# Layer 0 of a four-layer pre-activation network: where signed results, streamed statistics and weight preparation live and when they run

## The chip, the core and the metric

The kernel runs on one core of a Trainium2 chip. A core has five engines with an instruction stream of their own each: TensorE (PE, matmuls), VectorE (DVE), ScalarE (ACT), GpSimd (POOL) and SyncE (SP). SP and POOL also issue DMA transfers here, each in the order of its own stream. The metric is the device time of one execution in microseconds (us); the kernel before takes 2870.44 us, the median of three runs (2867.19 to 2876.09).

## The reference

The input `x` has shape (1024, 16, 16, 16), float32: batch, height, width, channel. Four layers follow, each `x = x + f(gn(x))`, where `gn` normalises over height, width and the two channels of each of eight groups:

- layer 0: `f` is a tensor-train product with three cores, a linear map from the 4096 values of one sample to 4096 values;
- layers 1 and 3: `f` is a cellular-automaton update: two fixed 3 x 3 depthwise filters, a dense layer from 48 to 128 with relu, a dense layer back to 16, and a mask from a 3 x 3 maximum;
- layer 2: `f` is a 3 x 3 convolution with 16 channels in and out, plus a bias.

All of the change lies in the code of layer 0 and in the preparation of later layers' weights, which runs beside layer 0.

## The kernel before

**Data.** The batch is worked on in two chunks of 512. Two big tiles in the on-chip memory, `XN[0]` and `XN[1]` (128 partitions x 32 lines x 512 values), take turns; `flats` are the same tiles as flat rows of 16384 values. The running sum of the network lies in DRAM as `xf[0]` and `xf[1]`, one for each chunk.

**Layer 0 as 13 pairs.** The tensor-train product is written as 13 pairs of smaller products (`OUTER`, a fast block-matrix scheme), numbered 0 to 12. Pair j has four units, q = 0 to 3, and each unit seven inner products (`INNER`) in two halves: 14 steps in a unit, 56 in a pair. One step is four float32 matmuls 128 x 128 x 256 at L1538, which the profile shows as two records each, so a pair has 448 such records. The order of work inside a unit is written out by hand in `pieces` (L1517): after given steps the code emits `store(u - 1)`, the VectorE operations that mix weight blocks (`mix`, L1454), `build(u + 1, h)` (L1427: PE matmuls at L1439 that make the next unit's weights, copied out by ACT at L1444) and `gload(u + 2, h)` (L1400: the DMA loads for the build after that, on SP). `gather` (L1568) adds the results of an inner product into the unit's tile `r`, on ACT (L1580, L1582) and VectorE (L1574, L1584). There are two places for `r`, so one unit's results are stored while the next unit's are gathered.

**Store.** `store(u)` (L1481) sends a unit's results to the places of `xf` where the scheme needs them, with signs: some as they are, some negated or as a sum of both results with signs. The latter are first made into a tile of the pool `t4`, by ACT (L1498) or VectorE (L1505, L1507). From the second time that a place of `xf` is written, the DMA accumulates and is issued by POOL (L1512); the first goes through SP (L1514).

**The part.** The input of pair p, its part, lies in tile `XN[p % 2]`: values 0 to 8191 hold lines that `part_steps` (L1192) builds during pair p - 1 from blocks in DRAM, fetched in pieces of two lines into `t4` (L1255), two pieces ahead, but one ahead for part 11 and none for part 12 (`deep`, L1219). Values 8192 to 14335, three eighths of the tile and here called its third, hold three sums of those lines. `combined` (L1162) makes them: five sums in two halves, ten VectorE operations (L1178). For the pairs in `late` (L2064: 1, 2, 4, 6, 8, 10, 12) they are woven into the first ten steps of the pair itself; for the others they run at the end of the pair before.

So when the next pair is in `late`, the third of the other tile stays unused for the whole of a pair. The weight preparation (`nca_weights`, L228) works in such a third: `rooms` (L2007) is the third of `XN[0]` for both sets.

**The pool `t4`.** Four tiles of 128 x 1024 float32, given out in turn. In layer 0 it serves the fetched pieces, the signed results, the pieces of the statistics, and the room of the filter weights. A tile that is asked for is written only when the users of its last content are done, a DMA out of it included.

**Beside a pair.** `run` (L1958) emits the 56 steps of a pair, and between them the callables of several lists ("spans"). Each span has a start and an end as a fraction of the pair; a bare number in the list is idle time in us of an assumed pair of 107 us, held to at most 0.7 of the span, and the rest is shared out to the callables by their costs. This fixes the place of every instruction in each engine's stream; on the chip each engine runs its stream in order and waits where data are missing. The lists beside pair j are:

- `part_steps(j + 1)`, from 0.04 to 0.78;
- `aside[j]`: weight set 1 in pair 3, its folding in pair 5, set 3 in pair 7, its folding in pair 9, the convolution's filter weights in pair 8, statistics in pairs 10 and 11;
- `share[j]` of the 32 residual steps (L1316): POOL accumulates 512 KB of the input from `xr` into `xf` (L1319).

**Statistics.** `ahead(kind, q, root)` (L883) reads a quarter of `xf[0]` back in four pieces (L890): kind 0 sums the pieces on VectorE (L906, L909), lets PE average (`pmean`, L806), ACT copy (L917) and SP store the mean to DRAM (`means`, L918); kind 1 fetches the mean (L894), subtracts it (L897), squares on ACT (L900), sums, and lets PE make the variance (`pvar`, L922). The loads are two pieces ahead. `roots_ahead` (L945) makes the reciprocal roots and spreads them (`pr`, L950). Pair 12 then loads `xf[0]` as the next layer's input and applies both.

**Weights.** A set (`inputs` to `store`, L254 to L331) is a chain of small DMAs on POOL, a few matmuls and POOL copies, ending in the stores of `L_conv_pk` and `L_conv_kp`. Folding (`fold`, L380) has 22 steps: matmuls (L403), ACT copies into one of three tiles (L409), and sends to DRAM, half of them on POOL and half on SP (L415). `conv_weights` (L440) issues 42 small DMAs on POOL in one block (L457, L465, L468) and spreads the result 60 us later.

Of the kernel before, what the change touches and what calls it, by code (L numbers as in the profile page):

```python
# [13 lines left out]
AF = mybir.ActivationFunctionType  # L14
# [7 lines left out]
P = 128  # L22
# [83 lines left out]
def conv_preact_kernel(ctx: ExitStack, tc: tile.TileContext, a: dict, out: bass.AP):  # L106
# [333 lines left out]
    def conv_weights():  # L440
# [3 lines left out]
        room = work([P, 2, NB], "t4", "convn").rearrange("p a b -> p (a b)")  # L444
# [4 lines left out]
        V.memset(room[:, 0:448], 0.0)  # L449
        V.memset(hw, 0.0)  # L450
        f = a["L2_conv_filters"]
        with nc.allow_non_contiguous_dma(reason="weights"):
            for w in range(8):
# [7 lines left out]
            for wh in range(2):  # L461
                for y in range(3):
                    for e in range(2):
                        r0 = 32 * (y + e)
                        G.dma_start(hn[r0 + wh : r0 + 32 : 2, wh, e], f[y, 2 - 2 * wh])  # L465
            for m in range(4):
                for v in range(2):
                    G.dma_start(  # L468
                        b2[32 * m + v : 32 * m + 32 : 2], a["L2_conv_bias"].unsqueeze(1)
                    )  # L470
# [7 lines left out]
        return spread  # L478
# [404 lines left out]
    def ahead(kind, q, root):  # L883

        st = {}
        rows = slice(32 * q, 32 * q + 32)

        def load(w):
            st[w] = work([P, 2, NB], "t4", "piece")
            nc.sync.dma_start(st[w], xf[0][w : w + 2, q].rearrange("w p b -> p w b"))  # L890

        def fetch():
            st["m"] = work([P, NB], "s", "m")
            nc.sync.dma_start(st["m"], means[q])  # L894

        def centre(w):
            V.tensor_tensor(  # L897
                st[w], st[w], st["m"].unsqueeze(1).broadcast_to([P, 2, NB]), ALU.subtract
            )
            A.activation(st[w], st[w], AF.Square)  # L900

        def add(w):
            x = st.pop(w)
            if w == 0:
                st["s"] = work([P, NB], "s", "s1s")
                V.tensor_tensor(st["s"], x[:, 0], x[:, 1], ALU.add)  # L906
                return
            for i in range(2):
                V.tensor_tensor(st["s"], st["s"], x[:, i], ALU.add)  # L909

        def mean():
            st["p"] = psum([P, NB], "pmean")
            average(st["p"], gm_cw, st["s"])

        def keep_mean():
            m = work([P, NB], "s", "m")
            A.copy(m, st["p"])  # L917
            nc.sync.dma_start(means[q], m)  # L918

        def var():  # L920
            st["v"] = psum([P, NB], "pvar")
            T.matmul(  # L922
                st["v"][rows], gv_cw.rearrange("p f j -> p (f j)"), st["s"], start=True, stop=True
            )

        def keep_var():
            if "ve" not in root:
                root["ve"] = work([P, NB], "n", "ve")
            V.tensor_scalar(root["ve"][rows], st["v"][rows], GN_EPS, None, ALU.add)

        def centred_too(w):
            return [(1.2, lambda: centre(w)), 1.5] if kind else []

        steps = [(0, fetch)] if kind else []
        steps += [(0, lambda: load(0)), (0, lambda: load(2)), 4]
        for w in (0, 2, 4, 6):
            steps += centred_too(w) + [(1.3 if w else 0.7, lambda w=w: add(w))]
            if w < 4:
                steps.append((0, lambda w=w: load(w + 4)))
            steps.append(1)  # L940
        if kind:
            return steps + [1, (0.6, var), 1, (0.4, keep_var)]
# [1224 lines left out]
```

## Time and profile before

| | |
|---|---|
| median of three runs | 2870.44 us (2867.19 to 2876.09) |
| the profiled execution, its own time | 2871.32 us |
| its span, first to last instruction | 2869.6 us |
| granted TensorE clock, mean | 0.978 |
| busy share of the span: PE, VectorE, ACT, POOL | 95%, 70%, 44%, 18% |
| layer 0's thirteen pairs | 47.1 to 1686.8 us |
| pairs 2 to 12, us each | 114.9, 124.9, 132.3, 130.2, 108.1, 110.6, 118.8, 132.1, 158.2, 125.5, 105.7 |

A line of a stretch gives its bounds and length, then for each engine the busy time and, in brackets, the number of instructions, then the granted clock (1.00 is full), the mean busy share of the 16 DMA engines and GB/s. A line of waits reads: engine, tile and line that waited; what it waited for; us in total, number of waits, longest. "SPq" is SyncE's DMA queue. A busy PE is a modelled figure, so a stretch is best judged by its length.

### The profile page before, as it was taken

The numbers are of one execution on the slowest core, as the hardware profiler recorded it, in microseconds if no ns is written. First come the engines' busy times: TensorE is split into PE (matmuls) and PEld (weight loads), VectorE is DVE, ScalarE is ACT, GpSimd is POOL, SyncE is SP. The second block draws the span as 40 slices with busy tenths as digits, with TensorE's granted clock in tenths as the row PEclk, the third lists the DMA queues.
The fourth block names the chain that finished last, engine by engine and source line by source line (L and its number), as shares of the span: only waits on it lengthen the run. The fifth ranks groups of instructions, "written<-read, shape, count | busy, mean of one in ns | idle before, by whom it ended". The sixth has DMA issues, their size and how long they took to land.

```text
span 2869.6 us, 48201 instructions
## 1 busy us (share of the span) xinstructions
PE 2722.4 (95%) x19342; PEld 1771.9 (62%) x19342; DVE 1999.9 (70%) x2440; ACT 1268.9 (44%) x2139; POOL 525.8 (18%) x666
## 2 busy tenths in 40 slices
PE   6998999879999999998898999999999999999997
PEld 5877888768788878876777863343333333333444
DVE  8595667656778767555676868757877777766654
ACT  3323222122432222341232236666768657676664
POOL 2000014622421454221011101111112221110000
PEclk8999999989999999999999999999999999999998
DMA  6685678898975687978576855456566867454665
GB/s 247 218 321 192 227 162 201 169 238 188 240 172 147 172 187 163 223 169 240 159 198 144 238 145 128 100 124 156 109 148 133 196 99 193 101 99 105 171 177 202
DMA packets 261536, 502.21 MB, mean 175 GB/s; under 512 B 29285, under 2 KB 96921, under 8 KB 252097
## 3 DMA queue, kind: packets, MB, share of 16 engines
q1 hardware_dynamic: 178896, 340.88, 35.7%
q0 software_dynamic: 82224, 158.12, 32.7%
q8 instruction: 153, 2.51, 0.4%
q14 instruction: 71, 0.57, 0.1%
q10 hardware_dynamic: 192, 0.13, 0.0%
HBM read 280.66 MB, written 223.35 MB: 176 GB/s over the span
## 4 chain that ended last, share of the span: by engine, by line
PE 72%; DMA 10%; DVE 9%; issue 5%; POOL 2%; ACT 1%; SPq 1%; DVEq 0%; POOLq 0%; ACTq 0%
PE po L1538 30%; PE ph L1945 20%; PE po L1774 8%; PE po L1629 5%; PE pw L1439 4%; DMA xf<-r 1%; DMA piece<-xf 1%; DMA xn<-xn 1%; DVE xn L1178 1%; DMA xf<-neg 1%; DVE xn L1149 1%; DMA xn<-in_x_dram 1%; DMA xf<-xr 1%; PE po L1638 1%; PE L_conv_pe L403 1%
## 5 line engine op out<-in xcount | busy, mean ns | idle before, releaser
L1538 PE MATMUL po<-xn,s 128*128 128x256 f32 x3328 | 774.7, 390 | 48.9 <-DVE s L1469 17.8
L1948 ACT ACTIVATE hid<-ph,pack 128x512 f32<-128x512 f32 (+1 forms) x1040 | 641.7, 684 | 312.9 <-PE ph L1945 253.6
L1538 PEld LDWEIGHTS po<-xn,s 128*128 128x128 f32 x3328 | 639.7, 195 | 165.7 <-issue 24.7
L1538 PE MATMUL po<-xn,w 128*128 128x256 f32 x2496 | 574.3, 385 | 4.5 <-DVE xn L1178 4.5
L1538 PEld LDWEIGHTS po<-xn,w 128*128 128x128 f32 x2496 | 471.9, 192 | 86.4 <-issue 10.3
L1945 PE MATMUL ph<-xn,wq 32*128 32x512 f32 (+1 forms) x3752 | 518.1, 590 | 1.9 <-DVE u L1786 1.5
L1444 ACT COPY w<-pw 128x512 f32<-128x512 f32 x416 | 213.6, 600 | 475.4 <-PE pw L1439 379.3
L1945 PEld LDWEIGHTS ph<-xn,wq 32*128 32x128 f32 x3752 | 233.8, 184 | 228.7 <-issue 209.8
L1469 DVE TENSOR_TENSOR s<-w 128x1024 f32<-128x1024 f32 x208 | 252.5, 1222 | 50.1 <-PE po L1538 46.8
L1945 PE MATMUL ph<-xn,pack 32*128 32x512 f32 x1288 | 273.7, 607 | 5.8 <-DVE u L1786 1.6
L1774 PE MATMUL po<-hid,pack 128*32 128x512 f32 (+1 forms) x2080 | 256.0, 592 | 0.8 <-ACT hid L1948 0.5
L1786 DVE SCALAR_TENSOR_TENSOR u<-po,pack,xn 128x512 f32<-128x512 f32 (+1 forms) x130 | 96.4, 741 | 168.1 <-PE po L1774 167.0
L1828 POOL DMA_DIRECT2D xf<-u x96 | 81.9, 853 | 619.4 <-DVE u L1826 587.0
L1178 DVE TENSOR_TENSOR xn<-xn 128x1024 f32<-128x1024 f32 x130 | 154.2, 1219 | 35.1 <-DMA L_conv_kp<-xn 35.1
L744 DVE TENSOR_TENSOR xn<-xn,m 128x1024 f32<-128x1024 f32 x128 | 150.3, 1219 | 34.7 <-ACT m L767 34.6
L1945 PEld LDWEIGHTS ph<-xn,pack 32*128 32x128 f32 x1288 | 115.0, 184 | 91.3 <-issue 63.4
L1629 PE MATMUL po<-xn,convw 128*128 128x512 f32 x368 | 163.6, 598 | 0.0
L1774 PEld LDWEIGHTS po<-hid,pack 128*32 128x32 f32 x2080 | 53.9, 109 | 174.9 <-ACT hid L1948 87.1
L1439 PE MATMUL pw<-R,gq 32*128 32x128 f32 x3328 | 144.5, 286 | 8.5 <-DVE small L1091 7.9
L1439 PEld LDWEIGHTS pw<-R,gq 32*128 32x128 f32 x3328 | 116.7, 188 | 43.4 <-issue 39.6
L1574 DVE TENSOR_TENSOR r<-r,po 128x1024 f32<-128x1024 f32 x78 | 95.0, 1218 | 69.5 <-PE po L1538 60.4
L1217 DVE TENSOR_TENSOR xn<-xn,piece 128x1024 f32<-128x1024 f32 x96 | 116.2, 1220 | 34.8 <-DMA piece<-xb 34.8
(222 smaller groups left out, 2814.6 us busy)
## 6 DMA issues: line engine op xcount, KB each, us to landing
xn<-xf SPq DMA_DIRECT2D x96, 512.0 KB
xn<-xb SPq DMA_DIRECT2D x36, 1024.0 KB
wq<-L_conv_wy SPq DMA_DIRECT2D x192, 192.0 KB
piece<-xb SPq DMA_DIRECT2D x64, 512.0 KB
xf<-xn POOLq DMA_DIRECT2D x48, 512.0 KB, 9.8
xf<-neg POOLq DMA_DIRECT2D x48, 512.0 KB, 9.7
xf<-r POOLq DMA_DIRECT2D x48, 512.0 KB, 11.4
xf<-u POOLq DMA_DIRECT2D x96, 256.0 KB, 4.2
```

The source lines that it names most:

```text
L744: V.tensor_tensor(part, part, m().unsqueeze(1).broadcast_to([P, 2, NB]), op)
L1178: V.tensor_tensor(out, y, z, f)
L1217: V.tensor_tensor(y, y, x(), ALU.add if sign > 0 else ALU.subtract)
L1439: T.matmul(pw[r][:, v, i], g[rows, P * (2 * v + i) : P * (2 * v + i) + P], R[rows, k], start=k == 0, stop=k == len(gs) - 1,)
L1444: A.copy(w.rearrange("p b s t m -> p (b s t) m")[:, :, 32 * r : 32 * r + 32].rearrange("p k (v o) -> p v k o", v=2), pw[r].rearrange("p v ...
L1469: V.tensor_tensor(t.rearrange("p s t m -> p (s t m)"), x, y, f)
L1538: T.matmul(po[:, i], matrix(u, what)[:, i, t], x, start=t == 0, stop=t == 3)
L1629: T.matmul(st["po", h][wh], conv["fw"][:, y], X[:, 16 * wh + h + y - 1], start=y == max(0, 1 - h), stop=y == min(2, S - h),)
L1774: T.matmul(po[32 * j : 32 * j + 32], nca["w1"][:, v], hid[j], start=v == 0, stop=v == 1)
L1786: V.scalar_tensor_tensor(u, po, nca["b1"], X[:, 8 * q + w2, cols(hf)], ALU.add, ALU.add)
L1945: T.matmul(ph, w, x, start=k == 0, stop=k == len(tiles) - 1)
L1948: A.activation(h, ph, AF.Relu, bias=nca["bt"][:, r : r + 1])
```

## The change

- `sent(u)` is new. In pairs 3, 4 and 5, for q = 0 to 2, a signed result is made in one of six slots of 1024 values in the third of the other tile instead of a `t4` tile. In other pairs, and for q = 3 (whose store falls into the next pair), it stays in `t4`.
- `late` holds all pairs from 1 to 12; nothing is combined at the end of a pair any more, and `part_steps` ends at 0.80.
- `rooms` are now both thirds; weight set 1 is prepared in pair 2 in the third of `XN[1]`, until 0.85, and folded in pair 6, until 0.92; set 3 stays in pair 7, in `XN[0]`, until 0.85, and is folded in pair 9, until 0.92.
- `conv_weights` works in the third of `XN[1]` in pair 8 and issues its DMAs in 19 steps with 2 us of idling after each.
- `ahead` takes all jobs of a pair at once. Pieces go through six slots in the third of the other tile, loaded three ahead across the jobs; each job adds its pieces into its first one and halves that at the end; the mean or variance of a job is taken after six entries of the next job's list.
- `gload` issues its narrow loads, eight for each half of a unit's weights and needed for pair 11 alone, on POOL instead of SP.
- `deep` is gone: pieces of every part are fetched two ahead.
- The residual steps are shared out anew: 3, 0, 3, 1, 4, 3, 1, 1, 2, 4 in pairs 2 to 11 and the last ten in pair 12 (before: 3, 3, 3, 2, 2, 2, 2, 3, 4, 4 and four).

```diff
-        room = work([P, 2, NB], "t4", "convn").rearrange("p a b -> p (a b)")
...
+        steps = [clear] + [lambda w=w: main(w) for w in range(8)]
+        steps += [lambda wh=wh, y=y: edge(wh, y) for wh in range(2) for y in range(3)]
+        steps += [lambda m=m: bias(m) for m in range(4)]
+        return [x for step in steps for x in (step, 2)] + [8, spread]
...
-    def ahead(kind, q, root):
...
-        def load(w):
-            st[w] = work([P, 2, NB], "t4", "piece")
-            nc.sync.dma_start(st[w], xf[0][w : w + 2, q].rearrange("w p b -> p w b"))
...
+    def ahead(jobs, root, room):
+        slots = [
+            room[:, 2 * NB * i : 2 * NB * i + 2 * NB].rearrange("p (w b) -> p w b", w=2) for i in range(6)
+        ]
+        todo = [(kind, q, w) for kind, q in jobs for w in (0, 2, 4, 6)]
+        def load(i):
+            if i < len(todo):
+                _, q, w = todo[i]
+                nc.sync.dma_start(slots[i % 6], xf[0][w : w + 2, q].rearrange("w p b -> p w b"))
...
+            def add(x):
+                V.tensor_tensor(first, first, x, ALU.add)
+            def last():
+                st["s"] = work([P, NB], "s", "s1s")
+                V.tensor_tensor(st["s"], first[:, 0], first[:, 1], ALU.add)
...
+            for i in range(i0, i0 + 4):
+                x = slots[i % 6]
+                if kind:
+                    steps += [(1.2, lambda x=x: centre(x)), 1.5]
+                if i > i0:
+                    steps.append((1.2, lambda x=x: add(x)))
+                if i == i0 + 3:
+                    steps.append((0.8, last))
+                steps += [(0, lambda i=i: load(i + 3)), 0.7]
...
+        steps = [(0, lambda i=i: load(i)) for i in range(3)] + [6]
+        end = []
+        for n, (kind, q) in enumerate(jobs):
+            body, more = job(kind, q, 4 * n)
+            steps += body[:6] + end + body[6:]
+            end = more
+        return steps + [5] + end
...
-        deep = {NP - 2: 1, NP - 1: 0}.get(j, 2)
...
-                            queue.dma_start(
-                                g[row : row + 16], g_dram[0][l % 2, q, h, o, l // 2]
-                            )
+                            G.dma_start(g[row : row + 16], g_dram[0][l % 2, q, h, o, l // 2])
...
+        def sent(u):
+            j, q = units[u]
+            if j not in (3, 4, 5) or q == 3:
+                return work([P, 2, NB], "t4", "neg")
+            st["sent"] = at = (st.get("sent", 0) + 1) % 6
+            lo = 8192 + 2 * NB * at
+            return flats[1 - j % 2][:, lo : lo + 2 * NB].rearrange("p (s n) -> p s n", s=2)
...
-                    have[c] = t = work([P, 2, NB], "t4", "neg")
+                    have[c] = t = sent(u)
...
-    rooms = [flats[0][:, 8192:14336]] * 2
+    rooms = [x[:, 8192:14336] for x in flats]
...
-        nca_weights(name, room) for name, room in zip(("L1_conv_", "L3_conv_"), rooms)
+        nca_weights(name, room) for name, room in zip(("L1_conv_", "L3_conv_"), rooms[::-1])
...
-        late = (1, 2, 4, 6, 8, 10, 12)
+        late = range(1, NP)
...
-        share = {2: 3, 3: 3, 4: 3, 5: 2, 6: 2, 7: 2, 8: 2, 9: 3, 10: 4, 11: 4, 12: 4}
+        aside = {
+            2: (set1, 0.85),
+            6: (fold1, 0.92),
+            7: (set3, 0.85),
+            8: (conv_weights(rooms[1]), 0.9),
+            9: (fold3, 0.92),
+            10: (ahead([(0, 0), (0, 1), (0, 2), (0, 3), (1, 0), (1, 1)], root, rooms[1]), 0.96),
+            11: (ahead([(1, 2), (1, 3)], root, rooms[0]) + roots_ahead(root), 0.96),
+        }
+        share = {2: 3, 4: 3, 5: 1, 6: 4, 7: 3, 8: 1, 9: 1, 10: 2, 11: 4}
```

## The prediction

> **What bounds the kernel now.** The page first: TensorE carries the chain that ended last, and the idle time in front of layer 0's main matmul is small.
>
> ```profile
> PE 72%; DMA 10%; DVE 9%; issue 5%; POOL 2%; ACT 1%; SPq 1%; DVEq 0%; POOLq 0%; ACTq 0%
> L1538 PE MATMUL po<-xn,s 128*128 128x256 f32 x3328 | 774.7, 390 | 48.9 <-DVE s L1469 17.8
> ```
>
> Then the stretches, one per pair (here pairs 3, 4, 6, 7, 8, 10, 11, 12), cut where a pair's first L1538 starts.
>
> ```profile
> core 0: us, PE busy (x) PEld busy (x) DVE busy (x) ACT busy (x) POOL busy (x), PEclk, DMA share, GB/s
> 440.40:565.30 124.90, 115.84 (x718) 96.70 (x717) 89.55 (x105) 29.33 (x54) 71.56 (x101) 0.96 0.88 196
> 565.30:697.60 132.30, 113.60 (x769) 96.77 (x768) 81.07 (x81) 29.02 (x52) 29.64 (x29) 0.91 0.86 199
> ...
> 827.80:935.90 108.10, 107.30 (x705) 92.21 (x704) 100.40 (x95) 26.17 (x49) 14.17 (x12) 1.00 0.68 176
> 935.90:1046.50 110.60, 110.60 (x717) 93.50 (x716) 74.71 (x93) 25.29 (x49) 58.74 (x93) 1.00 0.76 161
> 1046.50:1165.30 118.80, 112.37 (x769) 96.01 (x768) 89.57 (x94) 27.73 (x51) 42.77 (x62) 0.97 0.80 194
> ...
> 1297.40:1455.60 158.20, 129.44 (x909) 104.27 (x908) 104.40 (x117) 36.22 (x61) 14.84 (x13) 0.91 0.66 182
> 1455.60:1581.10 125.50, 118.18 (x718) 95.56 (x718) 87.98 (x103) 36.05 (x61) 17.07 (x15) 0.97 0.73 184
> 1581.10:1686.80 105.70, 104.88 (x641) 90.20 (x639) 91.93 (x84) 21.00 (x40) 14.62 (x13) 1.00 0.71 180
> ```
>
> Pairs 6 and 7 show the floor: 108.1 us for 705 matmuls without a gap. Another small weight-build matmul costs 0.035 us (pair 2: 898 in 114.9 us; (114.9 - 108.1)/193). Floors then: pair 3 110.6 (as pair 7, which also prepares a weight set), pairs 4 and 8 110.3, pair 10 118.5 and pair 11 112.1 (statistics matmuls at about 0.3 us), pair 12 105.9. Excess over floor: **14.3, 22.0, 8.5, 39.7, 13.4 us** in pairs 3, 4, 8, 10, 11, together 97.9 us. That is all this change can give back; PE idle time and its half-clock tails are both in it.
>
> What ends the waits in pairs 3 and early 4:
>
> ```profile
> DVE xn L1178 <- DMA L_conv_kp<-xn: 24.6, 1, 24.6
> ...
> ACT neg L1498 <- DVE xn L1217: 19.5, 1, 19.5
> ACT neg L1498 <- DMA xf<-neg: 17.3, 1, 17.3
> ...
> PE po L1538 <- ACT xn L1582: 15.1, 2, 11.2
> ...
> PE po L1538 <- DMA xf<-neg: 7.5, 1, 7.5
> ```
>
> ACT stands in front of a negated result because its t4 tile is still a piece not yet added (19.5), or a store not yet landed (17.3); the gathers behind it in ACT's order release PE late (15.1). VectorE waits 24.6 us to overwrite the third of the tile in which weight set 1 still has stores. In pair 10, the waits of the DMA queue SP and then of the engines:
>
> ```profile
> SPq L918 <- ACT m L917: 56.4, 4, 16.6
> ```
>
> ```profile
> PE pmean L806 <- DVE s1s L909: 19.0, 3, 9.3
> ...
> DVE piece L897 <- DMA piece<-xf: 12.6, 1, 12.6
> ...
> DVE s1s L906 <- DMA piece<-xf: 10.2, 1, 10.2
> ```
>
> SP stands 56.4 us in front of storing a mean; the next job's pieces are behind it, so VectorE sums late and PE waits for the sum.
>
> **The Trainium skill.** "Perfetto Trace Analysis", Optimization Strategy: the same gap repeating can mean that there isn't enough SBUF for the next tile; three pmean waits, up to 9.3 us, fit. "DMA: Bandwidth & Descriptors", Anatomy of one DMA: a semaphore wait is spent on the issuing sequencer before dispatch; SPq L918 shows it. Same page, Issuing engines are not separate DMA queues: moving issues frees sequencer time, not engines; no run here isolates it. "TensorE: Matmul & The Clock Gate", Part 1: an idle window of about 3.4 us halves the clock; pairs 4 and 10 at 0.91 agree, about 0.09 x 132.3 = 12 us of clock in pair 4 besides the gap.
>
> **The change, part by part.**
> Signed results in the idle third, pairs 3 to 5, q 0 to 2. Pair 3 makes three per unit, pair 4 one, pair 5 two; without q 3, which stays in t4, that is 9 + 3 + 6 = 18 moved. No instruction is added. Both ACT waits above (19.5 and 17.3) lose their t4 cause, and pair 4's pieces have t4 to themselves. Next in line is the second buffer of a unit's results: ACT waited 8.2 us (one L1580 wait on DMA xf<-xn) because POOL's stores were late; they are late because of set 1, which also leaves. The last slots must have landed before the next pair's sums write there: issued near step 44 of 56, six stores took 22 us from issue to the last landing in pair 3 (484 to 506), so about step 55; the write is at step 3 of the next pair, some 8 us later.
> Weight set 1 from pair 3 to 2, ending at 0.85 instead of 0.97 (set 3 too). Pair 2 takes set 1's 2.5 us of PE from pair 3: zero sum. POOL loses 57 DMAs of set 1 (51 in pair 3, six early in pair 4) and three accumulations there. The planner gives each of the set's ten callables an equal share of what idling leaves, 0.83 x 0.30 / 10 = 0.025 of the pair, so the storing step comes at 0.825, step 47 of 56, instead of 0.97 - 0.031, step 53: 12 us earlier, with less ahead of it; the 24.6 us wait and the 10.5 us one in pair 8 should vanish. POOL in pair 2 has 12 stores, set 1, three accumulations: much as pair 7, which shows no gap. I take 2 us of new waits, between 0 and 10.
> Fold 1 from pair 5 to 6, with 4 accumulations. 88 matmuls move, zero sum. Behind an accumulation waiting for a landing on POOL stand fold sends, and ACT's copies wait for their three tiles: 2 us, between 0 and 8.
> Combined lines always in the pair's own start (new in 3, 5, 7, 9, 11). Ten VectorE sums, 12.2 us (1.22 each), move to the first ten steps (about 20 us), which also hold three mixes and the gathers. Pairs 6 and 12 start so already and PE waits 0.8 us: 1.2 us each, at most 5. VectorE afterwards: pair 3 has 89.6 + 12.2 less set 1's 6, about 96 of 110, and pair 11 88.0 + 12.2 - 0.9, about 99 of 112; pair 6 ran 100.4 of 108.1 with 0.8 us of gap.
> Statistics streamed through six slots. Per job VectorE adds 3 x 1.22 + 0.69 = 4.35 instead of 7 x 0.69 = 4.8. Five pieces are on the way when SP stops at a mean, against none; the mean stands two sums later. 24 pieces of 512 KB remain. DMA was busy 0.66 x 158.2 = 104 us; two accumulations fewer (3.1 us each: POOL's queue in pair 12 took 40 us for 13) leave 98 of 121, share 0.81, as in pair 8. SP still stops at each mean until ACT has copied it, but what is next late is then the mean's place on PE, not the data. Excess left: 6 us in pair 10, between 2 (as pair 2) and 25 (pieces land 9 us after issue, as from 1306 to 1315, and every job waits for one: 6 x 4).
> Pair 11. Loads for its builds (64 small DMAs) go from SP to POOL: 64 x 0.5 = 32 us of POOL's issue (the filter loads take 0.49 to 0.84 each), hidden in POOL's idle 250 us of two pairs. With them goes SP's wait for the matmuls that free the weight buffer (L1423, 23.4 us in four waits, longest 12.6), now POOL's: behind it stand accumulations and the next unit's stores, and for those the second result buffer gives a unit, 27 us. Cost taken as nothing; bounds: a gain of 3 us where SP's pieces come sooner, a loss of 5; without the cover see the third rival. Pair 12's pieces are fetched two ahead. But its first 20 us now hold the sums (12.2), centring and adding (4 x 1.22) and three quarters of a unit's mixes and gathers (of 5 x 1.22 + 3 x 1.22 + 2 x 0.69 = 11), 25 us of VectorE: excess 8 instead of 13.4, between 3 and 16.
> Filter weights in pair 8, in steps, out of t4: the 42 DMAs stood in one block on POOL and PE never waited for them; nothing, 1 us either way. Six more accumulations in pair 12: 6 x 3.1 = 19 us raise DMA from 75 to 94 of 105.7; X0's 16 loads are needed one per 5.5 us and come at 2.7: nothing, up to 5.
>
> Sum: excess after 2 (pair 3), 2 (4), 1.5 (8), 6 (10), 8 (11) = 19.5, so 78.4 gained; costs 3 x 1.2 (pairs 5, 7, 9) + 2 + 2 = 7.6. Net 70.8. The profiled execution took 2871.3 us (span 2869.6), 0.9 above the median of 2870.44: 2871.3 - 70.8 = 2800.5, **2799.6 against the median**.
>
> **Rivals.** Streams starve (0.12): 24 pieces in 120 us come too late; pair 10 and 11 keep 40 of their 53 us: gain 78.4 - 26 - 7.6 = 45, 2826 us. For it: pieces took 9 us to land (1306 to 1315); against: SP runs ahead into six slots. POOL congestion moves (0.09): pairs 2 and 6 get pair 3's waits (14 and 22 us): 2799.6 + 32 = 2832. For it: in the trace POOL waits, in order, for the eighth DMA before, so eight are in flight at most; against: pair 7. Slower (0.05): build loads on POOL. They are issued about 12 steps, 23 us, before their build; POOL landings took up to 21 us in pair 3, 6 to 19 in pairs 10 and 11. Eight builds late by x us each cancel 71 us at x = 9, that is at landings above 32 us; at x = 11, 2887 us. It does nothing (0.03): if the ACT and SP waits only uncover equal DMA waits: 2870.
>
> **How the numbers follow.** Likeliest case 0.71: gain 45 to 98, own range 2773 to 2826, value 2799.6. Reaching to most of the two weaker gains gives 2770 to 2838. 0.3% (8.6 us) is about what a measurement can tell from no change. Faster 0.71 + 0.12 + 0.09 = 0.92, same 0.03, slower 0.05.
>
> **What would show it.** Right: pairs 3, 4, 8 within 3 us of floor, no L1178 wait on L_conv_kp, no ACT neg wait over 5 us; pair 10 at 121 to 128 with PEclk near 1.00. Wrong: pmean or pvar waits of over 3 us remain; PE waits on ACT in pairs 2 or 6; weight builds (L1439) in pair 11 waiting for gq; pair 12 above 110.

## The result, and the profile after

The changed kernel takes **2829.64 us** (median of four runs, 2823.28 to 2831.96) against 2871.5 us before: ratio 0.985, 95% interval 0.9828 to 0.9873, a gain of 42 us. The forecast gain was 71 us. The profiled execution took 2831.96 us, its span is 2830.1 us.

The page of the changed kernel, chain shares by engine and the main matmul's group (L1538 of before is L1563 here):

```profile
PE 77%; DVE 10%; DMA 6%; issue 4%; ACT 1%; SPq 1%; DVEq 0%; ACTq 0%; POOLq 0%
L1563 PE MATMUL po<-xn,s 128*128 128x256 f32 x3328 | 768.0, 388 | 36.2 <-DVE s L1485 31.4
```

POOL is gone from the chain (2% before) and the idle time ahead of the group fell from 48.9 to 36.2 us. But the part of it that waits for VectorE's weight mixes rose from 17.8 to 31.4 us. DMA's share of the chain fell from 10% to 6%.

The stretches, one for each pair from 2 to 12, with the columns explained above:

```profile
326.00:450.80 124.80, 117.83 (x910) 100.25 (x909) 80.13 (x97) 29.73 (x54) 54.19 (x92) 0.97 0.77 179
450.80:566.60 115.80, 111.22 (x706) 94.45 (x705) 92.85 (x87) 29.23 (x52) 25.62 (x21) 0.97 0.89 217
566.60:676.70 110.10, 109.16 (x769) 93.89 (x768) 70.86 (x71) 29.11 (x52) 24.78 (x21) 1.00 0.85 192
676.70:790.00 113.30, 112.69 (x897) 97.58 (x896) 90.31 (x85) 28.99 (x52) 20.35 (x17) 1.00 0.82 205
790.00:913.80 123.80, 123.14 (x794) 95.16 (x793) 90.61 (x85) 49.47 (x93) 38.75 (x54) 0.99 0.78 194
913.80:1025.70 111.90, 110.53 (x718) 93.47 (x717) 84.91 (x102) 25.28 (x49) 63.68 (x97) 1.00 0.81 181
1025.70:1134.60 108.90, 108.90 (x770) 94.10 (x769) 79.26 (x84) 27.82 (x51) 40.09 (x58) 1.00 0.79 190
1134.60:1263.80 129.20, 128.54 (x1050) 101.09 (x1049) 74.26 (x73) 52.43 (x96) 39.52 (x54) 1.00 0.77 196
1263.80:1397.20 133.40, 123.34 (x910) 102.14 (x909) 90.81 (x89) 36.23 (x61) 28.39 (x43) 0.95 0.73 207
1397.20:1541.80 144.60, 122.94 (x717) 97.34 (x716) 98.56 (x108) 35.80 (x61) 32.77 (x47) 0.94 0.63 158
1541.80:1647.70 105.90, 104.92 (x641) 90.23 (x639) 92.00 (x84) 21.00 (x40) 20.16 (x19) 1.00 0.88 209
```

Against the prediction's own sums (floor plus the excess or cost that it gave each pair; set 1's 2.5 us are moved from pair 3 to pair 2; pairs 5 and 6 are taken together because the folding moved from one to the other):

| pair | before | forecast | after | after less forecast |
|---|---|---|---|---|
| 2 | 114.9 | 119.4 | 124.8 | +5.4 |
| 3 | 124.9 | 110.1 | 115.8 | +5.7 |
| 4 | 132.3 | 112.3 | 110.1 | -2.2 |
| 5 and 6 | 238.3 | 241.5 | 237.1 | -4.4 |
| 7 | 110.6 | 111.8 | 111.9 | +0.1 |
| 8 | 118.8 | 111.8 | 108.9 | -2.9 |
| 9 | 132.1 | 133.3 | 129.2 | -4.1 |
| 10 | 158.2 | 124.5 | 133.4 | +8.9 |
| 11 | 125.5 | 120.1 | 144.6 | +24.5 |
| 12 | 105.7 | 105.7 | 105.9 | +0.2 |

The last column adds up to 31.2 us. Pairs 4 to 9 and 12 came out as forecast or better. Pair 11 is the one large miss: it is 19 us *longer* than before. Pairs 10 and 11 together went from 283.7 to 278.0 us only. So the gain of 42 us is in the main that of pairs 3, 4 and 8, which became 41 us shorter, less the 10 us by which pair 2 became longer.

In pairs 3 and 4 (450.8 to 676.7 us) the waits of the signed results changed their cause:

```profile
ACT xn L1523 <- DVE r L1599: 17.8, 2, 10.8
ACT xn L1523 <- DVE xn L1599: 17.1, 2, 8.8
ACT neg L1523 <- issue: 12.7, 2, 6.3
PE po L1563 <- DVE s L1485: 5.5, 3, 2.5
```

ACT now waits for L1599, the gathered result that it is to negate. The t4 piece (19.5 us) and the store out of t4 (17.3 us) no longer hold it. In these pairs TensorE waits neither for ACT nor for a store, and VectorE's 24.6 us wait for `L_conv_kp` is gone from the list.

In pair 2, where weight set 1 now is, a wait of TensorE is new:

```profile
DVE xn L1170 <- DMA xn<-xr: 9.7, 1, 9.7
PE po L1563 <- DVE xn L1199: 6.7, 1, 6.7
```

Pair 11, waits of SyncE's queue:

```profile
SPq L901 <- DVE s1s L923: 41.9, 1, 41.9
SPq L976 <- ACT m L975: 41.4, 4, 30.1
```

Pair 11, waits of the engines:

```profile
DVE xn L915 <- DMA m<-means: 17.5, 2, 11.2
PE po L1563 <- DVE s L1485: 10.1, 4, 5.1
PE po L1563 <- DVE xn L1199: 5.0, 3, 2.2
PE pr L971 <- ACT m L975: 3.4, 2, 2.7
PE pr L971 <- DVE r L803: 3.2, 1, 3.2
```

And its chain (start, length, what; parts):

```profile
1398.54 13.55 DMA m<-means
1413.25 2.35 DVE xn L1199 x2
...
1441.25 1.22 DVE s L1485
1443.55 10.69 DMA m<-means
...
1455.41 1.23 DVE s L1485
1456.77 5.79 PE po L1563 x16
```

Three things can be read there. First, SP stands 41.9 us at L901: the statistics load number 6 (counted from 0) goes into slot 0, and in slot 0 lies the running sum of the first job (a job is the mean or variance of one quarter), which is free only after `last` (L923). Second, the mean of the second job is fetched (L911) by SP behind that stand, at 1443.55; VectorE needs it at once, stands in front of L915, and the weight mix behind it (L1485) reaches TensorE at 1456.77. The first mean, fetched at 1398.54 among the loads of the next part, takes 13.55 us. Third, TensorE waits 3.2 and 3.4 us in the spreading of the reciprocal roots (L971). With the larger of TensorE's gaps come half-clock stretches, in which the trace's clock records grant half of the full clock: 3.4, 6.8 and 6.8 us long, at 1433.7, 1454.2 and 1512.2. Before the change the spreading (then L950) waited less:

```profile
PE pr L950 <- DVE r L795: 2.1, 1, 2.1
PE pr L950 <- ACT m L954: 0.7, 1, 0.7
```

Pair 10 shows the second pattern too, in small:

```profile
DVE xn L919 <- DMA xn<-xf: 12.5, 5, 4.1
DVE xn L915 <- DMA m<-means: 10.3, 2, 6.8
PE po L1563 <- DVE s L1485: 10.1, 2, 6.6
```

### The profile page after: what moved, and what is told of

The parts are those of the page before. It is cut to its first block, busy times and chain, and to the rows that moved or that the text cites. A ratio compares the mean times of both kernels' runs of the same rounds, so it can differ in the third digit from the quotient of the medians.

```text
span 2830.1 us, 48160 instructions
## 1 busy us (share of the span) xinstructions
PE 2711.1 (96%) x19342; PEld 1766.3 (62%) x19342; DVE 1995.3 (71%) x2416; ACT 1267.6 (45%) x2139; POOL 553.6 (20%) x730
## 4 chain that ended last, share of the span: by engine, by line
PE 77%; DVE 10%; DMA 6%; issue 4%; ACT 1%; SPq 1%; DVEq 0%; ACTq 0%; POOLq 0%
PE po L1563 34%; PE ph L1970 21%; PE po L1799 8%; PE po L1654 5%; PE pw L1455 4%; DMA m<-means 2%; DVE xn L1199 1%; DMA xn<-xr 1%; DVE s L1485 1%; PE po L1663 1%; DVE xn L1170 1%; DMA xn<-in_x_dram 1%; PE L_conv_pe L403 1%; DMA piece<-xb 1%; PE ptx L1863 1%
## 5 line engine op out<-in xcount | busy, mean ns | idle before, releaser
L1563 PE MATMUL po<-xn,s 128*128 128x256 f32 x3328 | 768.0, 388 | 36.2 <-DVE s L1485 31.4
L1563 PEld LDWEIGHTS po<-xn,s 128*128 128x128 f32 x3328 | 634.1, 193 | 151.3 <-issue 39.8
L1563 PE MATMUL po<-xn,w 128*128 128x256 f32 x2496 | 571.6, 384 | 13.3 <-DVE xn L1199 13.3
L1563 PEld LDWEIGHTS po<-xn,w 128*128 128x128 f32 x2496 | 470.7, 191 | 93.6 <-DVE xn L1199 13.7
L1485 DVE TENSOR_TENSOR s<-w 128x1024 f32<-128x1024 f32 x208 | 251.5, 1218 | 43.2 <-PE po L1563 39.8
L752 DVE TENSOR_TENSOR xn<-xn,m 128x1024 f32<-128x1024 f32 x128 | 150.3, 1218 | 34.7 <-ACT m L775 34.6
L1599 DVE TENSOR_TENSOR r<-r,po 128x1024 f32<-128x1024 f32 x78 | 95.0, 1218 | 99.1 <-PE po L1563 87.3
L1537 POOL DMA_DIRECT2D xf<-xn x69 | 90.0, 1791 | 249.8 <-DVE xn L1530 77.6
```

The lines of the kernel that those rows point to most:

```text
L752: V.tensor_tensor(part, part, m().unsqueeze(1).broadcast_to([P, 2, NB]), op)
L1485: V.tensor_tensor(t.rearrange("p s t m -> p (s t m)"), x, y, f)
L1563: T.matmul(po[:, i], matrix(u, what)[:, i, t], x, start=t == 0, stop=t == 3)
L1599: V.tensor_tensor(part, part, po.unsqueeze(2).broadcast_to([P, 2, 2, 256]), ALU.add)
```

## The experiments

Each was run beside the kernel before: 2871.57 us beside the first four, 2870.4 us beside the next four, 2871.74 us beside the last four. From L944 on, line numbers in the variants with the means fetched first are three to nine higher than in the changed kernel.

| run | us | ratio to before, 95% interval | pair 2 | pair 3 | pair 10 | pair 11 |
|---|---|---|---|---|---|---|
| the change | 2829.64 | 0.985 (0.9828 to 0.9873) | 124.8 | 115.8 | 133.4 | 144.6 |
| e1_rolling | 2823.05 | 0.9821 (0.9798 to 0.9843) | 122.6 | 112.5 | 134.3 | 137.0 |
| e2_means | 2816.12 | 0.9808 (0.9778 to 0.9838) | 123.8 | 111.0 | 133.3 | 133.8 |
| e3_both | 2813.45 | 0.979 (0.9765 to 0.9814) | 125.2 | 114.4 | 132.7 | 132.1 |
| e4_late_alone | 2872.99 | 1.0007 (0.9995 to 1.0019) | 115.3 | 125.4 | 146.1 | 132.2 |
| e5_set1_later | 2836.15 | 0.9885 (0.9869 to 0.9902) | 121.7 | 121.4 | 134.5 | 146.9 |
| e6_old_streams | 2821.57 | 0.9836 (0.9818 to 0.9855) | 124.7 | 110.2 | 143.2 | 129.9 |
| e7_loads_on_sp | 2828.92 | 0.9862 (0.9842 to 0.9883) | 122.7 | 110.0 | 134.0 | 150.3 |
| e8_no_centre | 2808.36 | 0.9789 (0.9769 to 0.9809) | 123.3 | 113.9 | 133.8 | 126.0 |
| e9_roots | 2802.54 | 0.9759 (0.9744 to 0.9773) | 123.4 | 114.4 | 134.2 | 119.5 |
| e10_means | 2804.74 | 0.9763 (0.9746 to 0.9781) | 122.1 | 114.6 | 126.5 | 130.9 |
| e11_all | 2793.15 | 0.9726 (0.971 to 0.9742) | 122.6 | 114.2 | 124.8 | 119.5 |
| e12_four | 2789.71 | 0.9715 (0.97 to 0.9729) | 123.7 | 111.2 | 119.4 | 122.9 |

### The running sum, handed from slot to slot

```diff
-            def add(x):
-                V.tensor_tensor(first, first, x, ALU.add)
+            def add(x, before):
+                V.tensor_tensor(x, before, x, ALU.add)
```

`before` is the slot of the piece ahead, and `last` halves the fourth piece's slot. The same adds, but slot 0 is free after the first of them.

> The changed kernel, with the sum of a job moving from slot to slot (each addition writes into the newer piece) instead of staying in the first slot; nothing is left out. In the changed kernel SyncE stood 41.9 us in pair 11 and 31.3 us in pair 10 in front of a load into that first slot. Accumulator theory (that stand delays the second mean and pair 12's pieces): no wait of SPq L901 on s1s over 5 us, the second mean is fetched about 6 us sooner, pair 11 falls from 144.6 to about 132, pair 10 by 2 to 5 us: 12 to 18 us faster than the changed kernel's 2829.6. Means theory (the means are fetched in the same step in which they are needed, whatever the slots do): at most 6 us faster, pair 11 still at 138 or more. VectorE theory (pair 11's start holds too many VectorE operations): within 3 us of the changed kernel.

```profile
SPq L901 <- DVE xn L919: 23.7, 1, 23.7
```

Pair 11 fell by 7.6 us, and SP's longest stand for a slot of the statistics there from 41.9 to 23.7 us. TensorE's gap of 5.1 us after the second mean is gone; those after the first mean stay. So the accumulator's place costs time, but it isn't the whole of it: 137.0 us lies between the two theories' 132 and 138, nearer to that of the means.

### Both means fetched first

```diff
-            steps = [(0, fetch)] if kind else []
+            steps = [(0, fetch)] if kind and not means_first else []
+            if means_first:
+                fetches.append((0, fetch))
...
-        return steps + [5] + end
+        return fetches + steps + [5] + end
```

(in pair 11 only)

> The changed kernel, with both means of pair 11 fetched at the head of its statistics, ahead of pair 12's lines and of the pieces; nothing is left out. Means theory: the two VectorE waits on m<-means (6.3 and 11.2 us) go, with PE waits of about 9 us and their half-clock tails: pair 11 from 144.6 to about 128, 15 us faster than 2829.6. Accumulator theory: the first wait goes (6 us), but pair 12's pieces stay behind the stand of 41.9 us; pair 11 at about 137. VectorE theory: waits move to the mixes, pair 11 stays at 140 or more.

```profile
SPq L901 <- DVE s1s L923: 36.5, 1, 36.5
```

Pair 11 fell by 10.8 us, although SP still stood 36.5 us for the slot. Then the stand by itself is not what holds TensorE; what was queued behind it, the fetch, is most of it. The fall is less than the means theory's (to about 128), and the total's 13.5 us is near its 15.

### Both

> Both edits together on the changed kernel; nothing is left out. If both causes count: pair 11 at 118 to 124, pair 10 at about 129, 22 to 30 us faster than 2829.6, about 2803, which is the prediction's value. If VectorE's load at the start of pair 11 is a cause of its own, pair 11 stays above 128 and the total above 2810.

```profile
1395.50:1527.60 132.10, 121.42 (x718) 96.68 (x717) 98.40 (x108) 35.91 (x61) 32.76 (x47) 0.95 0.70 175
PE pr L974 <- ACT m L978: 3.4, 2, 2.7
PE pr L974 <- DVE r L803: 3.2, 1, 3.2
```

Pair 11 is at 132.1 us, 12.5 below the change, less than the 7.6 + 10.8 of the two alone. They remove partly the same wait: TensorE's gaps in pair 11 add up to 21.7 us in the change, 16.3 and 13.4 with one edit and 10.7 with both. The clock adds to it: after the same waits in the roots this execution ran 13.7 us at half clock, those of the two single edits 6.8. No VectorE wait for a mean remains in pair 11. Some 12 us above the forecast of 120.1 remained. By the text above (pair 11 above 128, total above 2810) they would be VectorE's load; e8_no_centre and e9_roots test that.

### The sums at the start of a pair, alone

```diff
-        late = (1, 2, 4, 6, 8, 10, 12)
+        late = range(1, NP)
```

(in the kernel before)

> The kernel before with one line changed: the three sums are combined in the pair's own first ten steps for all pairs from 1 to 12, so newly for 3, 5, 7, 9 and 11; nothing is left out. By the prediction's step (1.2 us in each of five pairs) it is 6 us slower than before, 2877. VectorE theory: the start of a pair with much other VectorE work suffers most, pair 3 and 11 by 5 to 8 us each, in all 12 to 20 us slower. If the sums at the end of the pair before had been in the way too: within 3 us of before.

This part of the change makes no difference that can be told by itself: ratio 1.0007 (0.9995 to 1.0019). The interval ends at 5.5 us, so the 3.6 us that the prediction's sum charged are not excluded. By pairs it moves time: pair 11 takes 6.7 us more, since the sums are now in it, and pair 10, whose end they left, takes 12.1 us less; pair 8 takes 2.9 us more. So part of what pair 10 gained in the change (158.2 to 133.4) is this, and not streaming.

### Weight set 1 later in pair 2

```diff
-            2: (set1, 0.85),
+            2: (set1, 0.92),
...
-                spans.append((aside[j][0], 0.02, aside[j][1]))
+                spans.append((aside[j][0], 0.15 if j == 2 else 0.02, aside[j][1]))
```

> The changed kernel with weight set 1 spread over 0.15 to 0.92 of pair 2 instead of 0.02 to 0.85; nothing else moves. Landing theory: in the changed kernel the set's small strided loads are on the DMA engines together with the first 1 MB load of pair 3's part (L1228); that load lands 8 us later than before, VectorE waits 9.7 us for it at L1170 with the next pair-2 sums behind, and TensorE has a gap of 6.75 us. With the set 14 us later the L1170 wait goes back to about 5 us, pair 2 falls from 124.8 to about 118 us, total about 2823. Rival, VectorE theory: it is the set's copies and the combined sums that fill VectorE; then the gap and pair 2 stay within 2 us and the total at 2828 to 2831.

The landing theory was right on the wait, and wrong on pair 2 (about 118) and on the total. VectorE's wait in front of L1170 fell from 9.7 to 5.5 us (5.3 before the change), TensorE's gap after it from 6.75 to 3.68 us, and pair 2 by 3.1 us, to 121.7. What was left of the gap has another cause, on VectorE:

```profile
349.26 0.48 DVE L257 MEMSET xn<- 128x512 f32 x1
...
351.98 1.15 DVE L1170 TENSOR_TENSOR xn<-xn 128x1024 f32<-128x1024 f32 x1
353.06 2.33 DVE L1199 TENSOR_TENSOR xn<-xn 128x1024 f32<-128x1024 f32 x2
```

The set's eight clearing operations, 2.7 us, now stand between that load and the sums for which TensorE waits; in the change they ran before the wait for the load. So the rival had a part in it. And pair 3 grew by 5.6 us. The two stretches and one wait of pair 3:

```profile
325.20:446.90 121.70, 117.83 (x910) 99.98 (x909) 81.28 (x97) 29.63 (x54) 61.01 (x91) 0.99 0.70 165
446.90:568.30 121.40, 112.73 (x705) 95.52 (x704) 92.62 (x87) 28.90 (x52) 25.61 (x21) 0.96 0.90 222
```

```profile
DVE xn L1199 <- DMA L_conv_kp<-xn: 10.0, 1, 10.0
```

That is the wait that the kernel before had at the start of pair 4 (24.6 us), back as soon as the set ends at 0.92. The earlier end is thus what keeps it away, as the prediction worked out.

### The statistics as before

The old `ahead` (pieces in t4, two ahead within a job, jobs one after the other, ends at 0.97) and the old `deep`; all else of the change stays.

```diff
-            10: (ahead([(0, 0), (0, 1), (0, 2), (0, 3), (1, 0), (1, 1)], root, rooms[1]), 0.96),
-            11: (ahead([(1, 2), (1, 3)], root, rooms[0]) + roots_ahead(root), 0.96),
+            10: ([x for at in ((0, 0), (0, 1), (0, 2), (0, 3), (1, 0), (1, 1)) for x in ahead_old(*at, root)], 0.97),
+            11: (ahead_old(1, 2, root) + ahead_old(1, 3, root) + roots_ahead(root), 0.97),
```

> The changed kernel with the statistics of before: pieces in t4, two ahead within one job, jobs one after the other, spans to 0.97, and parts 11 and 12 fetched one and none ahead as before. Everything else of the change stays. Theory A, streaming as made earned nothing net: what pair 10 gains by it pair 11 loses, since the kernel with only the sums moved had 146.1 and 132.2 us there, together 278.3, and the changed kernel has 133.4 and 144.6, together 278.0. Then pair 10 is 143 to 149, pair 11 129 to 135, and the total stays at 2827 to 2833. Theory B, of the prediction: streaming is worth 25 us or more over the two pairs, so the total rises above 2850.

Its pairs 10 and 11:

```profile
1258.00:1401.20 143.20, 126.75 (x910) 103.31 (x909) 93.50 (x107) 36.32 (x61) 28.38 (x43) 0.94 0.69 193
1401.20:1531.10 129.90, 121.28 (x718) 96.83 (x717) 99.00 (x113) 36.22 (x61) 32.76 (x47) 0.95 0.72 178
```

On the two pairs theory A holds: 273.1 us, against 278.0 us with the streams. What streaming gave pair 10 (9.8 us) it took from pair 11 (14.7 us), and more. The total came out below the stated 2827 us: of the 11.7 us between the two profiled executions 4.9 lie in these two pairs and 5.6 in pair 3, which has the same instructions in both and took 110.2 us in this one and 115.8 in the change's.

### The narrow loads on SP again

```diff
-                            G.dma_start(g[row : row + 16], g_dram[0][l % 2, q, h, o, l // 2])
+                            queue.dma_start(g[row : row + 16], g_dram[0][l % 2, q, h, o, l // 2])
```

> The changed kernel with the narrow weight loads for pair 11's builds on SP again, as before, instead of POOL. Prediction's step: that move costs nothing, between a gain of 3 us and a loss of 5, so the total stays within 3 us of 2829.6. Rival, order on SP: SP now stands up to 41.9 us before a statistics load whose place a running sum holds, and build loads queued behind it on SP come late; then weight builds in pairs 10 and 11 wait for their loads, TensorE waits for the weights, and the total rises by 5 to 30 us.

2828.92 us: no difference that can be told, as the prediction had it ("taken as nothing"). In the profiles pair 11 is 5.7 us longer with the loads on SP, but TensorE's gaps in it are no larger (20.8 us in all against 21.7). The clock differs, 0.90 against 0.94: 30.7 us ran at half clock against 17.1, which loses 6.8 us. Pairs 2 and 3, which hold the same instructions in both kernels, are 7.9 us shorter. In the change POOL does take on the wait for the weight buffer, 33.6 us in six waits in pairs 10 and 11, yet in neither kernel does a weight build wait for its loads.

### Pair 11 with less for VectorE

```diff
-                V.tensor_tensor(x, x, m, ALU.subtract)
+                if q < 2:
+                    V.tensor_tensor(x, x, m, ALU.subtract)
```

(on top of e3_both; it leaves out the subtraction of the mean for quarters 2 and 3, eight operations)

> The kernel with the sum handed from slot to slot and both means fetched first (2813.5 us, pair 11 132.1), with the eight subtractions of the mean in pair 11 left out: the variances of quarters 2 and 3 are then those of uncentred values. It takes 8 x 1.22 = 9.8 us of VectorE and both waits for a mean out of pair 11. VectorE theory: what is left in pair 11 above 112 us is half VectorE, so pair 11 falls by 6 us or more to 126 or less, the TensorE gap of 2.9 us there goes and the total is 2807 or less. Rival, roots theory: the rest is the tail of reciprocal roots (waits of 3.2, 0.7 and 2.7 us at L974 and two half-clock stretches of 6.8 us, worth about 13 us), so pair 11 stays above 129 us and the total above 2810.

Pair 11 fell by 6.1 us to 126.0, at the bound of the VectorE theory; the total, 5 us lower, is 1.4 us above the bound that it gave. But the three waits in the roots stayed as they were, at 3.23, 0.70 and 2.66 us, so they don't depend on VectorE's load. Of the 6.1 us, 2.9 is the gap that went; 3.4 is the clock, because after the same waits the half-clock stretches were 3.4 us long here and 6.8 in e3_both. So VectorE's load is worth about 3 us and the theory met its bound with the help of the clock; the roots are the larger part.

### The roots spaced

```diff
-        steps = rstd(root) + [2]
+        steps = rstd(root) + [6]
         for q in range(4):
-            steps += [(0.6, lambda q=q: spread(q)), 1, (0.2, lambda q=q: keep(q)), 1]
+            steps += [(0.6, lambda q=q: spread(q)), 1, (0.2, lambda q=q: keep(q)), 3]
```

(on top of e3_both)

> The kernel with the sum handed on and both means fetched first (2813.5 us; pair 11 132.1), with more idling between the steps of the reciprocal roots: 6 us instead of 2 before the first spreading matmul, 3 instead of 1 after each copy. Roots theory: the three waits in front of L974 (3.2, 0.7 and 2.7 us) and the two half-clock stretches of 6.8 us after them (3.4 us lost in each) come from spreading matmuls placed too soon after what they need; spaced, they go, pair 11 falls by 8 to 13 us to 119 to 124, and the total to 2801 to 2806. Rival, VectorE theory: the roots are late because VectorE has no room; squeezing the statistics ahead of them makes those late instead, and the total stays above 2810.

As the roots theory had it: pair 11 falls by 12.6 us, the total by 10.9, with no instruction more or less. The stretch of pair 11, and what TensorE's matmuls still wait for in it:

```profile
1392.70:1512.20 119.50, 114.36 (x717) 93.04 (x716) 98.55 (x108) 35.94 (x61) 32.80 (x47) 1.00 0.76 193
```

```profile
PE po L1566 <- DVE s L1488: 5.1, 2, 2.8
```

No wait in front of the spreading matmuls is left, and the clock is full. VectorE has 98.55 us of work against 98.40 in e3_both, so it did have room: the list left too little time between a result and its reader. Of the 12.6 us, 6.6 are the waits and 6.8 the half clock after them, which cost 3.4 us more in e3_both's execution than in the change's; about 1 us went to other gaps.

### The means of pair 10 early

```diff
-                st["m"] = work([P, NB], "s", "m")
+                st["m"] = work([P, NB], "s" if means_first else "n", "m")
...
+            places.append(len(steps) - 6)
+        if means_first:
+            return fetches + steps + [5] + end
+        for n in range(len(fetches) - 1, -1, -1):
+            at = places[n + 2]
+            steps[at:at] = [fetches[n]]
```

(on top of e3_both; the fetches of the fifth and sixth job go into the third and fourth job's steps, and into another pool tag)

> The same kernel (2813.5 us; pair 10 132.7), with the two means of pair 10's centring jobs fetched more than a job earlier, into the two tiles of another pool tag. Means theory: in pair 10 VectorE stood 7.2 us before L915 for a mean, TensorE had a gap of 7.0 us right after it and a half-clock stretch of 6.8 us; with the mean early pair 10 falls by 7 to 10 us to 123 to 126, total 2803 to 2807. Rival, lateness of VectorE: its mixes behind the wait were late anyhow by the jobs' loads, the gap only shrinks by 2 us or less, total above 2810.

Pair 10 falls from 132.7 to 126.5 us and the total by 8.7 us, within the means theory's range; pair 10 itself ends 0.5 us above its range. The waits left there:

```profile
DVE xn L919 <- DMA xn<-xf: 8.7, 3, 3.3
PE po L1572 <- DVE s L1494: 5.1, 1, 5.1
```

What is left is mostly pieces that land late.

### All of it, and four pieces ahead

```diff
-        steps = [(0, lambda i=i: load(i)) for i in range(3)] + [6]
+        steps = [(0, lambda i=i: load(i)) for i in range(4)] + [6]
...
-                steps += [(0, lambda i=i: load(i + 3)), 0.7]
+                steps += [(0, lambda i=i: load(i + 4)), 0.7]
```

The first of these two kernels has e9, e10 and set 1 begun at 0.08; the second adds the edit above, which is only possible with the sum handed on.

> Both of these together, and weight set 1 begun at 0.08 of pair 2 instead of 0.02, its end as it was (0.85). If the causes are separate, the two gains add: 18 to 20 us off 2813.5, and pair 2 falls from 125 by 2 to 4 us: 2790 to 2794. If set 1's last stores again meet the sums at the start of pair 3, as with an end at 0.92, pair 3 grows by 4 us or more. If one gain only uncovers the next wait: 2800 or more.

> All of that, and the statistics' pieces loaded four ahead instead of three. Starving theory: in pair 10 VectorE waited 1.7 and 3.1 us for a piece (L919), with a TensorE gap of 3.9 us and a half-clock stretch after it; one more piece on the way takes these away, 3 to 6 us less than without it. Rival, order on SP: each load now stands behind a sum one step nearer, and the build loads and the next part's pieces queued behind it on SP come later; no gain, or a loss of up to 5 us.

The gains add: 2813.45 - 10.9 - 8.7 = 2793.8, measured 2793.15. Set 1's start at 0.08 changed nothing that can be told apart: pair 2 at 122.6 lies within the 122.1 to 125.2 us of the nine changed kernels that begin it at 0.02. With four pieces ahead, pairs 10 and 11:

```profile
1256.00:1375.40 119.40, 118.68 (x909) 99.04 (x908) 90.81 (x89) 36.03 (x61) 28.39 (x43) 1.00 0.78 231
1375.40:1498.30 122.90, 117.77 (x718) 95.59 (x718) 98.78 (x108) 36.16 (x61) 32.75 (x47) 0.97 0.74 189
```

Pair 10 is at its floor (118.5) plus 1, VectorE's wait for pieces is down to 4.7 us and TensorE's gap to 0.7. Pair 11 is 3.4 us longer than in e11_all, with the same gaps: two stretches of half clock. The total falls by 3.4 us, at the lower end of the starving theory's 3 to 6, to **2789.71 us**, ratio 0.9715 (0.97 to 0.9729): the best kernel of the study, 40 us ahead of the change.

## Why the prediction was right, and where it was wrong

The direction held and the time lies in the stated range, 2770 to 2838. It lies outside the likeliest case's own 2773 to 2826, by 4 us; the width that holds it had been added for two rivals, and what happened was neither of them. That much is luck. The likeliest value was 30 us too low, and the runs show which terms of the sum were mis-sized.

- **Signed results out of t4, pairs 3 to 5: right.** Pair 4 ended at its floor (110.1 against 110.3), with full clock where it had 0.91. Both ACT waits of before are gone. No run undid this part alone. Weight set 1 and three accumulations on POOL left pair 3 in the same change, so how the 31 us of pairs 3 and 4 are shared among these three is not shown.
- **Weight set 1 in pair 2: right on the wait removed, too small on the wait made.** The 24.6 us wait vanished because the set ends earlier; e5_set1_later brings 10 us of it back. "Much as pair 7, which shows no gap" was the step that failed. In pair 2 the set's first loads are under way together with the first 1 MB load of the next part, VectorE waits 9.7 us for that load instead of 5.3, and the sums behind it release TensorE 6.75 us late. I took 2 us; it was 7.4, and 4.7 to 7.8 in the nine profiles with the set begun at 0.02. Pair 3 came out 5.7 us over its forecast, but little of that is a property of the change: with the same instructions there pair 3 took 110.0 to 115.8 us in the profiles of this study.
- **Sums at the start of every pair: right in total, not by pairs.** Pair 7 grew by 1.3 us (1.2 forecast), pair 9 shrank by 2.9, and e4_late_alone shows no difference that can be told. But there the sums alone make pair 11 6.7 us longer and pair 10 12.1 shorter. Pair 11's forecast counted their 12.2 us of VectorE and still let its excess fall; and nearly half of pair 10's gain of 24.8 us is theirs.
- **Fold 1, the filter weights, the loads on POOL, six more accumulations in pair 12: right at about nothing.** Pairs 5 and 6 together took 1.2 us less than before, pair 8 is 1.4 us below the floor that I gave it, e7_loads_on_sp tells no difference, pair 12 took 105.9 us with the DMA engines at 0.88. The slower rival (builds late by landings on POOL) did not happen.
- **Streams, "excess left: 6 us in pair 10" and "8 in pair 11": the failed step.** They were 14.9 and 32.5 us. The step said that SP runs ahead into six slots. It does so only as far as the slot with a running sum in it, which stays taken for a whole job, and SP's next instruction, the fetch of a mean, stands behind that load in program order. I had counted the transfers that the change speeds up, and not the small one queued behind them. In the kernel before, the second fetch of pair 11 came two of the 56 steps ahead of its first use; in the change both fall into the same step, which the lists of the change would have told. By e6_old_streams the streaming, as made, earned nothing (273.1 us for the two pairs without it, 278.0 with it). The first rival had nearly this size (2826 us) but another mechanism: pieces that land late. Of that there was some, in pair 10 (3.4 us by the fourth piece ahead), but the means and the running sum come first.
- **The roots: not in the sum at all.** Before the change TensorE already waited there for 2.05 and 0.69 us, with a half-clock stretch of 3.4 us after the first. The statistics' new list put the spreading matmuls closer to what they need, and the waits came to 6.6 us (3.23, 0.69 and 2.66), with a half-clock stretch of 6.8 us after the first. Pair 11's 24.5 us over the forecast come out as 12.5 for the two orders (144.6 to 132.1) and 12.6 for the roots (132.1 to 119.5), each uncertain by the 3.4 us by which the half clock after the same waits differed between executions.
- **The signs.** Of those for being right, pairs 4 and 8 at their floors and no wait for `L_conv_kp` came. Pair 3 (5.2 us over its floor), ACT's waits under 5 us (10.8, for the result itself) and pair 10 (133.4 us at a clock of 0.95) did not. None of those for being wrong came: the list had no sign for a mean or a root that comes late.
- **Two readings.** The 12 us of clock in pair 4 "besides the gap" count time twice. The half-clock stretch there is 23.9 us long and some 15 us of it lie inside the two gaps of 11.2 and 7.5 us, so about 9 us of matmuls ran slow, 4 us lost. And 0.035 us for a weight-build matmul contains TensorE's idle time of pair 2 (two gaps of 0.91 us, against one of 0.8 in pair 6); without the gaps it is (113.1 - 107.3)/193 = 0.030, so the floors of pairs 4 and 8 were about 1 us too high. The first is not in the sum, the second hardly moves it.

With the sum handed on, the means fetched early, the roots spaced and the fourth piece ahead the kernel runs at 2789.71 us; the forecast for the change was 2799.6.

## What to carry to other kernels

When loads are streamed through a ring, follow every instruction of the issuing queue in program order, and ask for each ring slot who holds it longest: an accumulator kept in the ring blocks the ring for its whole life, and a small fetch queued behind that load is late for its reader. A fetch placed in the same step as its first use makes the reader wait for its landing, in part or in whole: in pair 11 VectorE stood 6.3 and 11.2 us for landings of 13.6 and 10.7 us. Count a wait of 3 us on TensorE with the half clock after it: each of the six in pairs 2, 10 and 11 of the change came with 3.4 to 10.2 us of it. And where a list is drawn up anew, look again at the dependent steps at its tail.

## What the hardware showed that I had not expected

- A mean of 256 KB took 13.55 and 10.69 us from issue to landing beside the loads of a part and the statistics' pieces. The Trainium skill, "DMA: Bandwidth & Descriptors", Anatomy of one DMA, gives a fit for transfers issued by GpSimd of 2 us plus the bytes at 436 GB/s, an estimate of 2.6 us for this size; these are issued by SP under load, and the measurement decides here.
- The half clock comes in steps: in layer 0's pairs of these records the stretches are 3.4, 6.8 or 10.2 us long, and one, in pair 4, 23.9 in the kernel before and 27.3 in e4_late_alone. Gaps of 2.38 and 2.75 us in pair 11 were followed by none in e9_roots and e11_all, and the same two gaps by one stretch each in e12_four. "TensorE: Matmul & The Clock Gate", Part 1, says that the window runs freely, so that it depends on where in it the work falls; that agrees, though its idle window of 3.4 us is longer than these gaps. It would explain why pair 6 of the changed kernels, with the same instructions and the same one gap of 0.66 us, took 122.1 us in five of these profiles and 123.7 or 123.8, with one stretch, in the others; 1.7 us is what one stretch of 3.4 us costs.
- With ten accumulations of 512 KB in pair 12 instead of four, the DMA engines' busy share there was 0.88 instead of 0.71, and the pair took 0.2 us more.
